# Every second one-hot matrix of the longest neighbour tile made by ScalarE instead of every fourth, with two changed distances in the instruction order

## The chip, the core and the metric

The kernel runs on one core of a Trainium2 chip. The core has five instruction queues that run side by side and each in its own order: TensorE (PE in the profile, with PEld for its weight loads), VectorE (DVE), ScalarE (ACT), GpSimd (POOL) and SyncE (SP, which only starts DMAs here). The metric is the device time of one execution in microseconds (us). Shown for the kernel before are 14 runs: median 7110.54 us, from 7096.17 to 7130.31 us.

## The reference: what is computed

There are 16 graphs of 1024 nodes, 64 features per node, a dense 1024x1024 weighted adjacency, and four layers, each ending in a residual addition and a layer normalisation. The first two layers are matrix products with the adjacency and a small perceptron. The last two, one after the other, do this for each node:

```
adj_d = adjacency with some neighbours taken out ("dilated", both directions)
vals  = x of the remaining neighbours of each node, sorted per feature
agg   = 0.25*q(0.25) + 0.5*q(0.5) + 0.25*q(0.75)     # interpolated quantiles
y     = (relu((x + agg) @ W1 + b1) @ W2 + b2) * mask
x     = layernorm(x + y)
```

A node has some ten to thirty neighbours left. So the heart of the work is: collect the neighbours' rows, sort them per feature, weigh three quantiles.

## The kernel before, in words

**Tiles.** For each graph the nodes are ordered by their number of neighbours and cut into eight tiles of 128 nodes. The tiles have fixed list lengths, `SIZES = (10, 11, 13, 14, 15, 17, 19, 33)` (L26); the last is the long tile. Rounds k = 0 to 17 pair graph k in its third layer (member 0) with graph k-2 in its fourth (member 1), so that both are sorted by the same VectorE instructions. Rounds 0, 1, 16 and 17 have one member.

**Short tiles (0 to 6).** GpSimd gathers neighbour rows from DRAM with indirect DMAs, one per list place, tile and member (`gather`, L361), into the buffer `got_s`, a ring of 60 places (`fetch`, L908). A gather can be issued when the places that it writes have been freed, that is, when an earlier tile has been sorted, weighed and added up.

**The long tile (7).** Its rows are not gathered but picked by TensorE (`fill`, L728; `pick`, L354). For list place i = 1 to 32 and each member, a one-hot matrix `hot` (128 x 1024, bf16) says where `place` equals i, and 24 pairs of weight load and matmul against the three bf16 parts of x write 64 columns of a PSUM tile `pgk`. Four places share half of `pgk`; ScalarE copies a half out to `got` (`empty`, L742) when the second place of the next four has been issued. Of each four one-hots three are made by VectorE, by one `is_equal`, and the one with i % 4 == 3 by ScalarE in two activations, `far = |place - i|` (L750) and `hot = relu(1 - far)` (L752); those are issued two places ahead. All one-hots take turns in `HOTS = 6` buffers, in the order in which they are asked for.

**Order of the work.** The order on VectorE, ScalarE and TensorE is written out by a small planner, `Weave` (L846). The sorting instructions of VectorE are the clock: `Metered` (L193) adds 0.13 us and one 960th of a us per element for each VectorE instruction, or one 3840th for a `tensor_scalar` whose large operands are all 16 bits wide. I call such a planned us a *unit*. All other work is written as generators; `yield n` means that the next piece is due n units later, times the work's pace. After every sorting instruction `catch_up` emits all pieces that have come due. `finish` forces a work to its end, and its due times no longer count then. The generators are: `features` (layers one and two), `lists` and `ordered` (neighbour lists, L486 and L633), `fill`, `weigh` (ScalarE multiplies the sorted places by weights, L773), and `finish_round` (L930), which runs the perceptron and normalisation (`finish`, L793, and `settle`, L371) of a round's members while the next round is sorted. `read_back` (L835) then loads the rewritten rows again.

A place of `fill` takes `yield 2.4`, so a fill is 31 x 2.4 = 74.4 units from its first one-hot to its last (the pace is 0.7 for k < 3). A round ends with the sort of its long tile.

In `finish`, each half of the perceptron is: transpose on TensorE, copy, first product, activation, second product `pd` (L816), then `yield 9` (L817) before VectorE adds `pd` to the bias.

Of the kernel before, what the change touches and what calls it, by code (L numbers as in the profile page):

```python
# [13 lines left out]
F16 = mybir.dt.float16  # L14
BF = mybir.dt.bfloat16
I32 = mybir.dt.int32
U8 = mybir.dt.uint8
AF = mybir.ActivationFunctionType
ALU = mybir.AluOpType
AX = mybir.AxisListType  # L20

P = 128
# [7 lines left out]
HOTS = 6  # L30
# [182 lines left out]
def adj_resnorm_kernel(ctx: ExitStack, tc: tile.TileContext, x, adj_t, nodemask, w01, b01, w02, b02,  # L213
                       w21, b21, w22, b22, w31, b31, w32, b32, out):
    nc = tc.nc
    B, N, C = x.shape
    NT = N // P
# [506 lines left out]
    def members(k):  # L724

        return [(m, b, entries[b]) for m, b in enumerate((k, k - 2)) if 0 <= b < B]

    def fill(k):  # L728

        while k and (k - 1, NT - 1) not in free:  # L730
            yield 1
        t = NT - 1
        size = SIZES[t]
        got = tails[k] = s.lists.tile([P, 2, size, C], F32, name="got", tag="got_l", bufs=1)
        for m, b, e in members(k):
            while e.parts[m] is None or e.xs[m] is None or e.place is None or e.none is None:
                yield 1
            nc.scalar.copy(got[:, m, 0, :], e.xs[m][:, t, :])
            waiting = None

            def empty():
                nc.scalar.copy(got[:, m, waiting[0] : waiting[0] + 4, :], waiting[1])  # L742

            for i in range(1, size):
                if i % 4 == 1:
                    first, pg = i, pgs[i // 4 % 2]
                if i % 4 == 1:

                    far = s.work.tile([P, NT, P], F16, name="far", bufs=1)
                    nc.scalar.activation(far, e.place, AF.Abs, bias=minus_k[:, i + 2 : i + 3])  # L750
                    by_act = s.lists.tile([P, NT, P], BF, name="hot", bufs=HOTS)
                    nc.scalar.activation(by_act, far, AF.Relu, bias=one_f, scale=-1.0)  # L752
                if i % 4 == 3:
                    hot = by_act
                else:
                    hot = s.lists.tile([P, NT, P], BF, name="hot", bufs=HOTS)
                    dve.tensor_scalar(hot, e.place, float(i), None, op0=ALU.is_equal)
                whole = i < LEAST[t]
                if not whole:
                    nc.tensor.matmul(pg[:, i - first, :], e.none,  # L760
                                     ident_b[: KW - 1, i - 1 : i].to_broadcast([KW - 1, C]), start=True, stop=False)
                pick(pg[:, i - first, :], hot, e.parts[m], whole)
                yield 2.4
                if i % 4 == 2 and waiting:
                    empty()
                if i % 4 == 0:
                    waiting = first, pg
            yield 5
            empty()
            yield 0.5  # L770
            e.filled[m] = True
# [21 lines left out]
    def finish(b, e, layer, agg):  # L793

        xc = e.xs[layer]
        w1s, b1c, w2s, b2r = mlps[layer]
        y = s.work.tile([P, NT, C], F32, name="y_m", bufs=1)
        dve.tensor_add(agg, agg, xc)
        yield 2
        for h in range(NH):  # L800
            pt = s.psum.tile([P, HALF], F32, name="pt", tag="m", bufs=1)
            for q in range(G):
                nc.tensor.transpose(pt[:C, q * P : (q + 1) * P], agg[:, h * G + q, :], ident)
            yield 7
            o_t = s.work.tile([C, HALF], F32, name="o_t", bufs=1)
            nc.scalar.copy(o_t, pt[:C])
            yield 3
            ph = s.psum.tile([P, HALF], F32, name="ph", tag="m", bufs=1)
            nc.tensor.matmul(ph[:H], w1s, o_t, start=True, stop=True)
            yield 7  # L810
            h_t = s.work.tile([H, HALF], F32, name="h_t", tag="o_t", bufs=1)
            nc.scalar.activation(h_t, ph[:H], AF.Relu, bias=b1c)
            yield 3
            pd = s.psum.tile([P, G, C], F32, name="pd", tag="m", bufs=1)
            for q in range(G):
                nc.tensor.matmul(pd[:, q, :], h_t[:, q * P : (q + 1) * P], w2s, start=True, stop=True)  # L816
            yield 9  # L817
            dve.tensor_add(y[:, h * G : (h + 1) * G], pd, b2r[:, None, :].to_broadcast([P, G, C]))
        dve.tensor_mul(y, y, e.mask[:, :, None].to_broadcast([P, NT, C]))
        dve.tensor_add(y, y, xc)  # L820
        xn = agg if layer else s.feat.tile([P, NT, C], F32, name="x3s", bufs=3)
        yield from settle(xn, y, "m")
        yield 1
        dst, rows = (out_rows_of, e.out_rows) if layer else (table[1][b % 3], e.rows)
        for t in range(NT):
            put = nc.gpsimd.indirect_dma_start(
                out=dst, out_offset=bass.IndirectOffsetOnAxis(ap=rows[:, t : t + 1], axis=0), in_=xn[:, t, :],
                in_offset=None)
            tc.declare_no_dep(put.ins, group=f"rows{layer}{b}", reason="they write different rows")
            tc.add_to_no_dep_group(f"rows{layer}{b}", put.ins)  # L830
        if layer == 0:
            e.xs[1] = xn
            weave.add(read_back(b, e, dst))
# [103 lines left out]
    def sort_round(k):  # L937

        if k >= 2:
            weave.finish(rounds[k - 2])  # L940
        filling = weave.add(fill(k), 4.0, 0.7 if k < 3 else 1.0)
        first = members(k)[0][0]
        which = slice(first, first + len(members(k)))
        agg = s.feat.tile([P, 2, NT, C], F32, name="agg")
        sums = []
        for t in (*reversed(range(NT - 1)), NT - 1):
            if t == NT - 1:
                weave.finish(filling)
                got = tails[k]
            else:  # L950
                n = order_of_tiles.index((k, t))
                fetch(n)
                got = gots[n]
            other = s.lists.tile([P, 2, SIZES[t], C], F32, name="other", bufs=1)
            pair = got[:, which], other[:, which]
            for is_max, d, v, i, j, to in usual[t]:
                dve.tensor_tensor(cut_pair(pair[to], v, d if is_max else 0), cut_pair(pair[i], v),
                                  cut_pair(pair[j], v, d), op=ALU.max if is_max else ALU.min)
                weave.catch_up()
                fetch()  # L960
            if len(sums) >= 2:
                weave.finish(sums[-2])
            sums.append(weave.add(weigh(k, t, got, agg, which)))
            weave.catch_up()
        if k:
            weave.finish(rounds[k - 1])
        rounds.append(weave.add(finish_round(k, agg, sums)))

    with ExitStack() as main:
        s.feat = main.enter_context(tc.tile_pool(name="feat", bufs=2))  # L970
# [305 lines left out]
```

## Time and profile before

| quantity | value |
|---|---|
| median of 14 runs | 7110.54 us |
| the profiled execution | 7098.59 us, with a span of 7096.8 us from first to last instruction |
| TensorE busy | 3917.4 us (55%) |
| VectorE busy | 4484.3 us (63%) |
| ScalarE busy | 2754.3 us (39%) |
| GpSimd busy | 3468.7 us (49%) |
| granted TensorE clock, mean | 0.682 |

No engine is full over the span, so the shares alone do not say what bounds. In the profile's groups of instructions, a row gives line, engine, operation, written tile and read tiles, shapes, count, then the busy time and the mean duration in ns, then the engine's idle time just before these instructions and what ended it. "issue" means that the engine waited for nothing that the profile shows; "remote" that the releasing instruction was not found. In the windows view each row is a stretch of the span with the busy time of each engine in it, and the number of instructions in brackets.

From round 3 on the rounds repeat almost exactly every 420 us. The stretch from 3062 to 3482 us is one of them: the fill of member 0 from 3062 to 3213 us, that of member 1 from 3213 to 3335 us, and from there to 3482 us the rest, with the sort of the long tile at its end.

### The profile page before, as it was taken

What the parts mean: (1) busy time and instruction counts of PE and PEld (TensorE: products, weight loads), DVE (VectorE), ACT (ScalarE), POOL (GpSimd) and SP (SyncE); (2) the same over time, 40 slices, a digit from 0 to 9 for tenths busy, and PEclk for the clock granted to TensorE, in tenths of its full rate; (3) what the DMA queues carried; (4) which work ended last, traced back from release to release, by engine and by line L of the source; (5) the groups of instructions that cost most, each with busy time, mean ns of one, the idle gap of its engine ahead of it and who ended that gap; (6) DMA issues with size and microseconds to landing.
All of it is one profiled execution on the core that took longest, in us unless ns stands there. A gap on an engine that the chain in (4) does not pass through costs nothing.

```text
span 7096.8 us, 109051 instructions
## 1 busy us (share of the span) xinstructions
PE 3917.4 (55%) x43478; PEld 2890.8 (41%) x43512; DVE 4484.3 (63%) x8771; ACT 2754.3 (39%) x6304; POOL 3468.7 (49%) x3229
## 2 busy tenths in 40 slices
PE   7657565465655656566565654746465564523233
PEld 5435344243443434444344443524344443413222
DVE  1456456657557485665858566585755748576666
ACT  4235153434435353443534334353443535322222
POOL 0342525546455464544645455464545646566353
PEclk8777676676766767676676766767676676755555
DMA  3111212111111111111111111111111111001000
GB/s 87 39 39 48 55 25 55 31 30 45 39 44 36 36 44 30 44 39 42 32 36 45 33 44 35 44 35 32 41 38 44 35 36 21 19 18 22 11 20 11
DMA packets 420598, 259.24 MB, mean 37 GB/s; under 512 B 106590, under 2 KB 368878, under 8 KB 420078
## 3 DMA queue, kind: packets, MB, share of 16 engines
q0 software_dynamic: 102400, 105.06, 7.9%
q1 hardware_dynamic: 317678, 147.12, 7.5%
q8 instruction: 342, 5.60, 0.3%
q14 instruction: 178, 1.46, 0.1%
HBM read 239.37 MB, written 12.58 MB: 36 GB/s over the span
## 4 chain that ended last, share of the span: by engine, by line
DVE 34%; PE 30%; issue 18%; another core or an unknown queue 11%; ACT 7%; POOL 0%; DMA 0%; DVEq 0%; ACTq 0%; POOLq 0%
DVE other L207 12%; PE pgk L358 11%; DVE got L207 7%; DVE got_s L207 6%; PE pk L607 5%; PE pa L465 3%; PE px L434 3%; DVE best L207 2%; PE ordered_x L358 1%; ACT junk L585 1%; PE pd L816 1%; DVE less L207 1%; DVE hot L207 1%; PE pr L520 1%
## 5 line engine op out<-in xcount | busy, mean ns | idle before, releaser
L362 POOL DMA_INDIRECT got_s<-table,idx x2944 | 3149.7, 1070 | 3348.0 <-DVE other L207 877.6
L358 PEld LDWEIGHTS <-hot 128*128 128x128 bf16 x24576 | 1092.5, 112 | 1817.4 <-issue 1477.7
L358 PE MATMUL pgk<-x3p,hot 128*128 128x64 bf16 x12288 | 691.1, 220 | 780.8 <-issue 483.3
L358 PE MATMUL pgk<-x2p,hot 128*128 128x64 bf16 x12288 | 619.7, 210 | 703.5 <-issue 437.0
L207 DVE TENSOR_SCALAR hot<-place 128x1024 bf16<-128x1024 f16 x768 | 335.0, 439 | 1038.7 <-remote 547.4
L742 ACT COPY got<-pgk 128x256 f32<-128x256 f32 x256 | 95.0, 371 | 2197.6 <-PE pgk L358 1518.7
L607 PE MATMUL pk<-near,order 128*128 128x512 f16 x2048 | 530.6, 413 | 44.0 <-issue 41.5
L520 PE MATMUL pr<-steps,near 128*128 128x512 bf16 x1502 | 423.1, 445 | 235.2 <-ACT junk L526 165.1
L207 DVE TENSOR_TENSOR other<-got_s 128x512 f32<-128x512 f32 (+8 forms) x900 | 511.5, 582 | 37.3 <-ACT got_s L925 17.5
L207 DVE TENSOR_TENSOR got_s<-got_s 128x384 f32<-128x384 f32 (+6 forms) x918 | 493.0, 539 | 21.1 <-DVE hot L207 0.9
L465 PE MATMUL pa<-x,adj_r 128*128 128x65 f32 x2048 | 395.1, 369 | 72.1 <-issue 35.8
L781 ACT ACTIVATE got_s<-got_s,wts 128x64 f32<-128x64 f32 x1568 | 398.9, 336 | 71.1 <-DVE got_s L207 55.2
L564 PE MATMUL pv<-minus_n,takes 128*128 128x128 bf16 x1024 | 248.6, 265 | 300.5 <-DVE takes L207 295.8
L207 DVE TENSOR_TENSOR got_s<-other 128x512 f32<-128x512 f32 (+8 forms) x774 | 407.5, 539 | 8.7 <-DVE other L207 0.8
L465 PEld LDWEIGHTS pa<-x,adj_r 128*128 128x128 f32 x2048 | 379.1, 284 | 73.9 <-issue 45.8
L520 PEld LDWEIGHTS <-near 128*128 128x128 f16 x1536 | 168.6, 111 | 482.6 <-issue 361.2
L563 PE MATMUL pv<-scaled,near 128*128 128x128 f16 x1024 | 250.1, 266 | 171.2 <-ACT near L568 164.8
L607 PEld LDWEIGHTS <-order 128*128 128x128 bf16 x2048 | 205.3, 105 | 322.6 <-issue 148.3
L434 PE MATMUL px<-adj_r,x_s 128*64 128x128 f32 x2048 | 310.2, 309 | 47.1 <-issue 41.9
L207 DVE TENSOR_TENSOR other<-other 128x128 f32<-128x128 f32 (+13 forms) x558 | 318.7, 571 | 17.4 <-issue 0.8
L564 PEld LDWEIGHTS <-takes 128*128 128x128 bf16 x1024 | 121.2, 118 | 500.7 <-DVE takes L207 327.0
L526 ACT ACTIVATE junk<-pr,nb_st 128x1024 f16<-128x1024 f32 x256 | 282.0, 1108 | 64.9 <-PE pr L520 63.0
(202 smaller groups left out, 7413.3 us busy)
## 6 DMA issues: line engine op xcount, KB each, us to landing
adj_r<-in_adj_dram SPq DMA_DIRECT2D x256, 512.0 KB
got_s<-table,idx POOLq DMA_INDIRECT x2944
x_s<-in_x_dram SPq DMA_DIRECT2D x16, 256.0 KB
table<-x SPq DMA_DIRECT2D x16, 256.0 KB
x<-table SPq DMA_DIRECT2D x16, 256.0 KB
table<-x3s,rows POOLq DMA_INDIRECT x128
out_dram<-agg,out_rows POOLq DMA_INDIRECT x128
table<-no_row SPq DMA_DIRECT2D x6, 0.2 KB
```

Of the source, the lines that this page charges most:

```text
L207: return call(*args, **kwargs)
L358: nc.tensor.matmul(dst, hot[:, c, :], parts[:, c, q, :], start=first and c + q == 0, stop=c == NT - 1 and q == 2)
L362: nc.gpsimd.indirect_dma_start(out=dst, out_offset=None, in_=tab, in_offset=bass.IndirectOffsetOnAxis(ap=rows, axis=0))
L434: nc.tensor.matmul(px[C:, q * P : (q + 1) * P], x_s[:, jt, :], adj[t][:, jt, :], start=jt == 0, stop=jt == NT - 1)
L465: nc.tensor.matmul(pa[:, q, :], adj[i][:, jt, :], x1[:, jt, :], start=jt == 0, stop=jt == NT - 1)
L520: nc.tensor.matmul(pr[:, h * HALF : (h + 1) * HALF], near[:, c, t * P : (t + 1) * P], steps[:, ONSET + h * HALF - c * P :][:, :HALF], star ...
L526: nc.scalar.activation(junk, prs[t - 1], AF.Sign, bias=lim[:, i, t - 1 : t], scale=-1.0, accum_out=cut_at[:, i, t - 1 : t])
L563: nc.tensor.matmul(pv[:, cols], near[:, c, rows], scaled[:, c, :], start=True, stop=False)
L564: nc.tensor.matmul(pv[:, cols], takes[:, c, rows], minus_n, start=False, stop=False)
L607: nc.tensor.matmul(cols, order[:, c, t * P : (t + 1) * P], left(c, slice(h * G, (h + 1) * G)), start=c == 0, stop=c == NT - 1)
L742: nc.scalar.copy(got[:, m, waiting[0] : waiting[0] + 4, :], waiting[1])
L781: nc.scalar.activation(prods[:, m, i, :], got[:, m, slot_id, :], AF.Copy, scale=e.wts[:, t, i : i + 1])
```

## The change

The one-hots of all odd places (i % 2 == 1) are made by ScalarE, 16 per fill instead of 8; VectorE makes 16 instead of 24. They are asked for up to two places ahead: at place 1 the order is hot 3, hot 1, hot 2; then 5, 4, 7, 6 and so on. In the perceptron's second product `yield 9` becomes `yield 13`. The `finish_round` of rounds 15, 16 and 17 gets a pace of 0.7 (lag 0.0 is the default).

```diff
+    def by_act(i):
+        return i % 2 == 1
...
+            hots = {}
+
+            def make(i):
+
+                hots[i] = s.lists.tile([P, NT, P], BF, name="hot", bufs=HOTS)
+                if by_act(i):
+                    far = s.work.tile([P, NT, P], F16, name="far", bufs=1)
+                    nc.scalar.activation(far, e.place, AF.Abs, bias=minus_k[:, i : i + 1])
+                    nc.scalar.activation(hots[i], far, AF.Relu, bias=one_f, scale=-1.0)
+                else:
+                    dve.tensor_scalar(hots[i], e.place, float(i), None, op0=ALU.is_equal)
+
             for i in range(1, size):
                 if i % 4 == 1:
                     first, pg = i, pgs[i // 4 % 2]
-                if i % 4 == 1:
-
-                    far = s.work.tile([P, NT, P], F16, name="far", bufs=1)
-                    nc.scalar.activation(far, e.place, AF.Abs, bias=minus_k[:, i + 2 : i + 3])
-                    by_act = s.lists.tile([P, NT, P], BF, name="hot", bufs=HOTS)
-                    nc.scalar.activation(by_act, far, AF.Relu, bias=one_f, scale=-1.0)
-                if i % 4 == 3:
-                    hot = by_act
-                else:
-                    hot = s.lists.tile([P, NT, P], BF, name="hot", bufs=HOTS)
-                    dve.tensor_scalar(hot, e.place, float(i), None, op0=ALU.is_equal)
+                for ahead in range(i + 1, min(i + 3, size)):
+                    if by_act(ahead) and ahead not in hots:
+                        make(ahead)
+                if i not in hots:
+                    make(i)
+                hot = hots[i]
...
-            yield 9
+            yield 13
             dve.tensor_add(y[:, h * G : (h + 1) * G], pd, b2r[:, None, :].to_broadcast([P, G, C]))
...
-        rounds.append(weave.add(finish_round(k, agg, sums)))
+        rounds.append(weave.add(finish_round(k, agg, sums), 0.0, 0.7 if k >= B - 1 else 1.0))
```

## The prediction

> **What bounds the kernel now.** I read the page's shares first, then the chain that ended last. No engine is full, and the chain changes hands all the time: a third is VectorE work, a third TensorE work, and 29% is time in which nothing named was waited for.
>
> ```profile
> PE 3917.4 (55%) x43478; PEld 2890.8 (41%) x43512; DVE 4484.3 (63%) x8771; ACT 2754.3 (39%) x6304; POOL 3468.7 (49%) x3229
> ...
> DVE 34%; PE 30%; issue 18%; another core or an unknown queue 11%; ACT 7%; POOL 0%; DMA 0%; DVEq 0%; ACTq 0%; POOLq 0%
> ```
>
> Second, one steady round of 420 us cut into the two fills and the rest (windows view; the 29 us left out lie between the last two rows).
>
> ```profile
> 3062.00:3213.00 151.00, 101.87 (x1265) 71.18 (x1265) 81.69 (x161) 54.66 (x109) 67.67 (x66) 0.76 0.15 33
> 3213.00:3335.00 122.00, 68.78 (x904) 58.93 (x903) 67.77 (x138) 39.84 (x92) 65.13 (x65) 0.67 0.17 40
> 3364.00:3482.00 118.00, 55.14 (x383) 34.08 (x384) 113.66 (x183) 75.15 (x189) 68.44 (x51) 0.69 0.16 37
> ```
>
> The third busy column is VectorE: about half full in the fills, full (113.66 of 118) after them. So the fills go at TensorE's pace and the rest at VectorE's. Third, the waits over the span:
>
> ```profile
> PEld L358 <- issue: 1511.4, 1364, 31.3
> ...
> DVE hot L207 <- remote: 547.4, 80, 23.3
> DVE hot L207 <- PE pgk L358: 482.0, 75, 21.8
> ...
> PE pgk L358 <- ACT got L742: 267.1, 80, 31.2
> ...
> DVE y_m L207 <- PE pd L816: 236.4, 33, 11.4
> ...
> DVE y_m L207 <- remote: 89.6, 10, 21.3
> ...
> PE pgk L760 <- ACT got L742: 79.2, 57, 9.4
> ```
>
> VectorE waits 1029 us for a free one-hot buffer, that is, for TensorE. TensorE, where its records show a gap, mostly waits for nothing ("issue"). The timeline shows when: while GpSimd issues gathers back to back, TensorE starts only a few instructions per us; elsewhere it does the 24 pairs of one place in 0.9 us (at 3213.2, for one).
>
> ```profile
> 3156.09 0.94 POOL L362 DMA_INDIRECT got_s<-table,idx  x1 [0.30 <-issue]
> ...
> 3157.20 0.32 PE L358 MATMUL pgk<-x2p,hot 128*128 128x64 bf16 x3 [1.17 <-issue]
> ...
> 3157.34 0.94 POOL L362 DMA_INDIRECT got_s<-table,idx  x1 [0.30 <-issue]
> ...
> 3157.93 0.23 PE L358 MATMUL pgk<-x2p,hot 128*128 128x64 bf16 x1 [0.41 <-issue]
> ```
>
> Whether the gathers cause this I can't show; they go together here.
>
> **The change, part by part.** The sum is made against the profiled execution (7098.59 us, of which 1.8 lie outside the span); it is 12 us below the median of the 14 runs, and I apply the difference to that median.
>
> ```profile
> L207 DVE TENSOR_SCALAR hot<-place 128x1024 bf16<-128x1024 f16 x768 | 335.0, 439 | 1038.7 <-remote 547.4 <-PE pgk L358 482.0 <-issue 8.9
> ...
> L750 ACT ACTIVATE far<-place,minus_k 128x1024 f16<-128x1024 f16 x256 | 294.5, 1150 | 2.9 <-DVE place L207 2.4
> L752 ACT ACTIVATE hot<-far,one_f 128x1024 bf16<-128x1024 f16 x256 | 294.0, 1148 | 9.9 <-remote 1.6
> ```
>
> (1) *VectorE loses work.* 32 fills x 8 = 256 one-hots x 335.0/768 = 0.436 us: 112 us. They stand in the fills, where VectorE has time, but the planner moves the gain: a one-hot counts 0.13 + 1024/3840 = 0.397 units, a fill stays 74.4 units long, so 3.2 units of sorting move into each fill and leave the full stretch, which runs at about one us per unit. 32 x 3.2 = 102 us. Bounds: 0 and 112. I take -102. The Trainium skill's page "Perfetto Trace Analysis" (Identifying Performance Opportunities) says that improving a kernel generally means improving its most-contended engine, which by occupancy is VectorE; by it alone the term would be the whole 112 and the forecast 10 us lower. The windows disagree: in the fills relief of VectorE buys nothing by itself.
>
> (2) *Sorting brings its gathers along.* In the round GpSimd works 219.5 us beside 274.9 us of VectorE (sums of the same view over 3062 to 3482), 0.8 us per us, so 3.2 units bring 2.55 us, or 3.4 us with the 0.30 gaps (1.25 us a gather for 0.94 busy). If TensorE stood still in all of it: 32 x 3.4 = 109 us back; if in none: 0. In the two fills TensorE's matmul row is idle 102 of 273 us; its waits for named instructions are 27 (16.1 for `got`, 7.0 for a one-hot, 4.2 for `junk`), so 75 us of standing beside 133 x 1.25/0.94 = 177 us of gather time, 42%. I take 42% of 109, +46.
>
> (3) *The first one-hot.* Place 1 was made by VectorE in 0.43 us; now ScalarE makes hot 3, then hot 1, and TensorE waits for the last of four activations.
>
> ```profile
> 3061.99 1.15 ACT L750 ACTIVATE far<-place,minus_k 128x1024 f16<-128x1024 f16 x1
> 3063.17 1.15 ACT L752 ACTIVATE hot<-far,one_f 128x1024 bf16<-128x1024 f16 x1
> ```
>
> At 1.18 us a piece the fourth ends at 3066.7; TensorE began the fill at 3062.3. That is 4.4 us later, with the next graph's `px` products (L434) queued behind. In a round's second fill TensorE came to place 1 only at 3221.9 us, when ScalarE's four would just have ended (from 3216.8), so 18 first fills count: 0 to 79 us. TensorE has 20 us a round of named waits later in the fills that can take up such a delay; I take a quarter, +20. If ScalarE were busy at that place, its backlog would come on top.
>
> (4) *Later odd one-hots.* 256 x 2.298 = 588 us more for ScalarE, 18.4 us a fill. It is busy 54.7 of 151 and 39.8 of 122 us there, so it fits; without that room it would cost all 588. But hot 4n+5 now stands in ScalarE's queue behind the copy of places 4n-3 to 4n, which waits for TensorE, and behind it stand copies, `junk` and `weigh` for VectorE. From that copy (0.37) and two activations (2.3) to TensorE's need lie four places, 4 x 0.9 us at its quickest. Lower bound 0; upper 2.3 each. The nearest row is the one-hots ScalarE makes now: TensorE waited 9.0 us in all for 256 (5.4 weight loads, 3.6 matmuls). I take the same, +9. The page "TensorE: Matmul & The Clock Gate" (Architectural detail) calls ScalarE's queue strict FIFO, so a late copy would hold each such one-hot: by that rule alone, as an estimate, 256 x up to 2.3, 589 us instead of 9. The trace bears the waiting out (`got` copies waited 1518.7 us for TensorE), but the lateness after it is not in it.
>
> (5) *Buffers.* With every fourth one-hot made early, VectorE's place 4n+2 needed the buffer of 4n-1: a reach of three places. Now an even place needs the buffer of six places earlier, a ScalarE one that of four before its time. VectorE's 155 buffer waits can shrink by 3 x 2.4 = 7.2 us each, but TensorE is behind there anyway and the next instruction waits (`deg`, 17.6 us at 3365). Bounds: 0 to -108 (half of 30 fills x 7.2). Taken: a part of the 346 us in which TensorE in turn waits for `got`, 1.5 us in 15 rounds, -22.
>
> (6) *Perceptron.* 43 waits of 326 us for `pd`, each at most 4 us shorter: up to -172, were they not in the fills (3119, 3193, 3317 us in this round), where the next one-hot would wait instead: 0. The end of each member's work moves 8 units back: its eight indirect DMAs on POOL's queue, and for member 0 the read-back on SP's. The next round's gathers need two more short tiles freed before that, and the fill needs the read-back a round later: nothing. Without that cover, 8 us x 14 rounds, 112 us.
>
> (7) *Last rounds.* A member's finish takes 87 units, now 95 x 0.7 = 66.5. Graph 15's rows, written from 6820 us, come up to 20 us earlier, so the last gathers (6834 to 6900) crowd the last fill (from 6870) less. Bounds -25 and +30 (16 shortened distances by up to 2 us); no wait for `pd` in that stretch is over 3.1 us, so the gain is nearer: -12.
>
> Sum: -102 + 46 + 20 + 9 - 22 + 0 - 12 = -61; 7110.5 - 61 gives 7050.
>
> **The rivals.** *The gathers take it all back:* (2) at its upper bound: -102 + 109 + 20 + 9 - 22 - 12 = +2, 7112 us. For it: the timeline above. Against it: 58% of gather time in the fills goes with TensorE running. *ScalarE becomes what TensorE waits for* (slower): place, hot 4n+5 and hot 1; price 0.3 us for each of the 256 (77) and the full 79 of (3): -102 + 46 + 79 + 77 - 22 - 12 = +66, 7177 us. It decides once both together exceed 90 us instead of my 29. For it: L781 and `junk` stand in the same queue. Against it: 9.0 us now. *The longer reach pays:* (5) at -108: 7050 - 86 = 6964 us. For it: 1029 us of buffer waits. Against it: no work for TensorE goes away.
>
> **How the numbers follow.** Forecast 0.50, its own range 6985 to 7095; gathers 0.14; ScalarE 0.24; reach 0.12. This kernel's runs tell about 0.2% (14 us) from no change. Faster: 0.48 + 0.03 + 0 + 0.12 = 0.63; same: 0.02 + 0.08 + 0.01 = 0.11; slower: 0.03 + 0.23 = 0.26. The range goes from 6930 (the reach's 6964 with (1) at 112 and (7) at -25, rounded down) to 7175, which leaves out about half of ScalarE's case and a third of the reach's.
>
> **What would show it.** (1) VectorE's one-hots x512, some 223 us; full stretch about 6 us shorter per round. (2) More "issue" beside the gathers in the fills. (3) and (4) In the waits, TensorE for `hot` L752-like rows from ScalarE: under 60 us right, over 120 us the ScalarE rival. (5) VectorE's waits for `hot` well under 1029 us, with others grown. (6) `pd` waits smaller, the round no shorter for it. (7) Gathers of the last round before 6815 us. I'd be wrong if a round of about 414 us doesn't appear, above all by a slower start of the fills.

## The result: slower by 1%

The changed kernel takes 7191.43 us (median of 10 runs, 7170.56 to 7208.3), the kernel before beside it 7119.73 us (47 runs): a ratio of 1.0099, with a 95% interval of 1.0082 to 1.0117. That is 72 us slower, clear of no change, where 61 us faster was forecast, and above the range's end of 7175. The profiled execution took 7164.88 us, with a span of 7163.2.

First the page's shares of the changed kernel, then its one-hot rows among the groups of instructions.

```profile
PE 3929.6 (55%) x43477; PEld 2913.8 (41%) x43512; DVE 4387.7 (61%) x8515; ACT 3316.7 (46%) x6816; POOL 3495.4 (49%) x3229
...
L207 DVE TENSOR_SCALAR hot<-place 128x1024 bf16<-128x1024 f16 x512 | 220.4, 431 | 1250.2 <-remote 657.4
L755 ACT ACTIVATE hot<-far,one_f 128x1024 bf16<-128x1024 f16 x512 | 587.9, 1148 | 16.7
...
L754 ACT ACTIVATE far<-place,minus_k 128x1024 f16<-128x1024 f16 x512 | 586.7, 1146 | 5.9 <-DVE place L207 2.4
```

The work moved as costed: VectorE's one-hots fell from 335.0 to 220.4 us (223 expected), ScalarE's rose by 586 us (588). VectorE is less busy and the kernel is slower. The waits of the changed kernel say who waits now (us in total, times, longest):

```profile
DVE hot L207 <- remote: 657.4, 65, 27.4
...
DVE hot L207 <- PE pgk L358: 554.4, 81, 28.7
...
PEld L358 <- ACT hot L755: 374.3, 61, 95.3
POOL table L836 <- ACT x3s L388: 358.8, 31, 27.1
...
DVE best L207 <- ACT code L618: 280.2, 31, 61.8
...
PE pgk L770 <- ACT got L745: 202.7, 61, 16.0
PE pgk L358 <- ACT got L745: 193.2, 71, 20.7
```

The rows of before that answer to these:

```profile
POOL got_s L362 <- ACT got_s L781: 514.5, 98, 14.8
...
PEld L358 <- DVE hot L207: 198.5, 28, 96.0
...
DVE best L207 <- ACT code L618: 93.0, 19, 59.3
POOL table L826 <- ACT x3s L388: 92.5, 25, 31.9
...
PEld L358 <- DVE agg L207: 88.8, 1, 88.8
```

Before, weight loads waited 5.4 us for ScalarE's one-hots and 198.5 for VectorE's; `best` waited 93.0 us for `code`, and GpSimd's writes into `table` 92.5 us for `x3s`. TensorE's waits for ScalarE's copy `got` have two rows: at `e.none`'s product (L760 before, L770 now) they rose from 79.2 to 202.7 us, at the one-hot products (L358) they fell from 267.1 to 193.2, together 346 before and 396 now. Two long waits, at the starts of the fills of rounds 15 and 16, are in both kernels and only change their names: before 96.0 us for a VectorE one-hot and 88.8 for `agg`, now both for a ScalarE one-hot:

```profile
6455.53 2.69 PE L358 MATMUL pgk<-x2p,hot 128*128 128x64 bf16 x47 [94.17 <-ACT hot L755]
```

```profile
6803.04 1.20 PE L358 MATMUL pgk<-x3p,hot 128*128 128x64 bf16 x19 [95.21 <-ACT hot L755]
```

Without these two TensorE's weight loads wait 185 us for ScalarE's one-hots, and 219 us for one-hots of both engines, where it was 108 before.

The steady round that answers to the one shown of before, as windows (length, then busy us of PE, PEld, DVE, ACT, POOL, granted clock, DMA share, GB/s): first fill, second fill, the rest.

```profile
3120.00:3273.00 153.00, 93.47 (x1200) 69.19 (x1201) 80.06 (x157) 69.24 (x118) 77.14 (x75) 0.71 0.16 35
3273.00:3403.00 130.00, 85.48 (x969) 68.66 (x968) 68.26 (x137) 62.34 (x117) 62.90 (x60) 0.62 0.15 36
3403.00:3540.00 137.00, 76.36 (x550) 54.39 (x551) 120.10 (x198) 75.60 (x192) 84.61 (x66) 0.65 0.19 44
```

Before: 151, 122 and 147 us. The rest is 10 us shorter (step (1) expected 6), and the fills are 10 us longer. The round is 420 us again, not 414. The granted clock is lower in this round, but over the span it is 0.679 against 0.682.

So the 66 us between the two traces are mostly not in the steady rounds. The starts of the fills, changed kernel minus before (from the first one-hot of each in the two traces):

```
fill (round)    2 (2)  4 (3)  8 (5)  14 (8)  20 (11)  26 (14)  31 (17)  end
whole change    +12    +13    +49    +58     +70      +54      +89      +66
```

49 us are lost before round 5, 5 us in the nine rounds after it, and the remaining 12 in the last rounds. I had costed one steady round and multiplied.

### The profile page after: what moved, and what is told of

Same layout as the page of the kernel before. It is cut to its first block, busy times and chain, and to the rows that moved or that the text cites. A ratio compares the mean times of both kernels' runs of the same rounds, so it can differ in the third digit from the quotient of the medians.

```text
span 7163.2 us, 109625 instructions
## 1 busy us (share of the span) xinstructions
PE 3929.6 (55%) x43477; PEld 2913.8 (41%) x43512; DVE 4387.7 (61%) x8515; ACT 3316.7 (46%) x6816; POOL 3495.4 (49%) x3229
## 5 line engine op out<-in xcount | busy, mean ns | idle before, releaser
L362 POOL DMA_INDIRECT got_s<-table,idx x2944 | 3177.3, 1079 | 3105.5 <-ACT got_s L791 794.9
L358 PEld LDWEIGHTS <-hot 128*128 128x128 bf16 x24576 | 1079.9, 112 | 1908.2 <-issue 1451.8
L358 PE MATMUL pgk<-x2p,hot 128*128 128x64 bf16 x12288 | 637.6, 213 | 754.3 <-issue 410.1
L358 PE MATMUL pgk<-x3p,hot 128*128 128x64 bf16 x12288 | 647.1, 216 | 631.2 <-issue 411.6
L207 DVE TENSOR_SCALAR hot<-place 128x1024 bf16<-128x1024 f16 x512 | 220.4, 431 | 1250.2 <-remote 657.4
L755 ACT ACTIVATE hot<-far,one_f 128x1024 bf16<-128x1024 f16 x512 | 587.9, 1148 | 16.7
L754 ACT ACTIVATE far<-place,minus_k 128x1024 f16<-128x1024 f16 x512 | 586.7, 1146 | 5.9 <-DVE place L207 2.4
L465 PE MATMUL pa<-x,adj_r 128*128 128x65 f32 x2048 | 425.9, 377 | 176.5 <-issue 149.8
L207 DVE TENSOR_TENSOR got_s<-got_s 128x256 f32<-128x256 f32 (+6 forms) x918 | 491.0, 538 | 34.8 <-remote 12.7
L465 PEld LDWEIGHTS pa<-x,adj_r 128*128 128x128 f32 x2048 | 409.0, 295 | 186.4 <-issue 158.5
L207 DVE MAX8 best<-code 128x8 f16<-128x1024 f16 x112 | 136.9, 1222 | 329.7 <-ACT code L618 280.2
L836 POOL DMA_INDIRECT table<-x3s,rows x128 | 142.3, 1112 | 388.9 <-ACT x3s L388 358.8
```

The source lines that it names most:

```text
L207: return call(*args, **kwargs)
L358: nc.tensor.matmul(dst, hot[:, c, :], parts[:, c, q, :], start=first and c + q == 0, stop=c == NT - 1 and q == 2)
L362: nc.gpsimd.indirect_dma_start(out=dst, out_offset=None, in_=tab, in_offset=bass.IndirectOffsetOnAxis(ap=rows, axis=0))
L465: nc.tensor.matmul(pa[:, q, :], adj[i][:, jt, :], x1[:, jt, :], start=jt == 0, stop=jt == NT - 1)
L755: nc.scalar.activation(hots[i], far, AF.Relu, bias=one_f, scale=-1.0)
L836: put = nc.gpsimd.indirect_dma_start(out=dst, out_offset=bass.IndirectOffsetOnAxis(ap=rows[:, t : t + 1], axis=0), in_=xn[:, t, :], in_off ...
```

## The experiments

The theories: *S*, ScalarE's share: what TensorE needs from ScalarE, one-hots and copies, comes later. *G*: the sorting and gathers that the planner moves into the fills cost more there than the rest of the round gains. *N*: the moving is worth nothing either way. *D*: the longer perceptron distance delays the next rows. Kernels that were run together share their chip and their runs of the kernel before. The chip matters, as will be seen, so each group names its time for the kernel before.

### The parts alone (kernel before: 7107.67 us)

**The one-hots alone**: the change with these two lines put back.

```diff
-            yield 13
+            yield 9
...
-        rounds.append(weave.add(finish_round(k, agg, sums), 0.0, 0.7 if k >= B - 1 else 1.0))
+        rounds.append(weave.add(finish_round(k, agg, sums)))
```

> The one-hots changed alone; the distance in the perceptron (9) and the pace of the last rounds (1.0) as before. Theory S (ScalarE: what TensorE waits for, and what else stands in ScalarE's queue, comes later): this part alone carries the loss, ratio 1.007 to 1.015, TensorE's waits for one-hots of ScalarE over 200 us. Theory D (the longer distance in the perceptron delays the rows of the next layer): ratio 0.990 to 1.002 here, since the one-hots by themselves would gain as forecast.

Measured 7215.18 us, ratio 1.0157 (1.0129 to 1.0184): +108 us. So the one-hots by themselves carry the loss, and more than all of it.

**The distance alone.**

```diff
-            yield 9
+            yield 13
```

> The distance 13 in the perceptron alone. Theory S: 0.997 to 1.003, the waits for the second product shorter and others longer by as much. Theory D: 1.006 to 1.015, with the GpSimd queue waiting longer for the rewritten rows (92.5 us before, 358.8 us after the whole change).

Measured 7047.89 us, ratio 0.9913 (0.988 to 0.9945): -60 us, and the quickest kernel of this study on such a chip. Theory D falls here. VectorE's waits for `pd` fall from 326 us to 21; others of its waits grow, that of `best` for `code` from 93 to 190 us and that of `counted` for `pn` from 47 to 164. In the steady rounds each second fill begins 5 to 15 us sooner after the first. The fills' starts run ahead from round 6 on: -20 us at fill 14, -56 at fill 26, -59 at the end.

**The last rounds' pace alone.**

```diff
-        rounds.append(weave.add(finish_round(k, agg, sums)))
+        rounds.append(weave.add(finish_round(k, agg, sums), 0.0, 0.7 if k >= B - 1 else 1.0))
```

> The pace 0.7 of the last three finish rounds alone. Both theories: nothing changes up to round 15; ratio 0.996 to 1.000, a gain of 0 to 25 us after 6700 us. If the last rounds carry the loss instead, 1.003 or more.

Measured 7104.91 us, ratio 1.0003 (0.9984 to 1.0022): no change that can be told from nothing.

**The one-hots alone, but place 1 made by VectorE**, so 17 of the 32 are VectorE's. In this expectation "272 more instead of 256 fewer" is a slip of mine: VectorE makes 17 x 32 = 544 instead of 768.

```diff
-        return i % 2 == 1
+        return i % 2 == 1 and i > 1
```

> As the one-hots alone, but place 1 of each fill is again made by VectorE (272 more instead of 256 fewer on VectorE: it makes 17 of 32, ScalarE 15). If the late start of the fills (4.4 us in each of the 18 first fills) is what costs, this gives back 40 to 80 us against the one-hots alone, ratio to before near 1.000. If the loss lies in ScalarE's queue within the fills, it gives back under 20 us.

Measured 7184.18 us, ratio 1.0104 (1.0079 to 1.013). Place 1 is worth 31 us of the 108 by the medians; the intervals of the two ratios just overlap, so the size is rough. The waits of this kernel show what it gained and what stayed:

```profile
POOL got_s L362 <- ACT got_s L791: 932.7, 112, 24.1
...
DVE best L207 <- ACT code L618: 272.1, 30, 63.6
...
PE pgk L770 <- ACT got L745: 163.1, 73, 17.2
...
PE pgk L358 <- ACT got L745: 158.6, 61, 7.6
...
PEld L358 <- DVE hot L207: 139.3, 46, 93.8
...
PEld L358 <- ACT hot L755: 72.1, 43, 4.5
```

Without the one wait of 94 us, TensorE's weight loads now wait 118 us for one-hots of both engines, against 108 us in the kernel before. So they wait hardly longer for the matrices than before, and 76 us of loss stay. What stays high is `best` for ScalarE's `code` (before 93.0), the gathers for ScalarE's weighing of `got_s` (before 514.5) and `table` for `x3s` (331.4, before 92.5). TensorE's waits for the copy `got` are not among them: their two rows make 322 us, less than the 346 before.

Multiplied, the three parts make 1.0157 x 0.9913 x 1.0003 = 1.0072; the whole was 1.0099. With the intervals given, that is consistent with adding up. By stage they don't add up: from fill 8 to fill 26 the one-hots alone lose 19 us against before and the distance alone gains 66, but the whole change loses 5.

### Less for VectorE, more for ScalarE, each alone (kernel before: 6930.8 us)

**224 of VectorE's one-hots left out** (places 5, 9, ... 29 reuse the matrix before).

```diff
-                else:
+                elif i % 4 != 1 or i == 1:
                     hot = s.lists.tile([P, NT, P], BF, name="hot", bufs=HOTS)
                     dve.tensor_scalar(hot, e.place, float(i), None, op0=ALU.is_equal)
```

> 224 of VectorE's 768 one-hots are left out of the kernel before (places 5, 9, ..., 29 reuse the matrix of the place before, so those places fetch the wrong neighbour); nothing goes to ScalarE. It is step (1) with step (2) and without (3) and (4). By the prediction's steps: 7/8 of -102 and 7/8 of +46, about -50 us, ratio 0.993. Theory N (the gain of step (1) is not there: the rest of a round shortens, and the fill grows by as much because TensorE's work and the gathers are what they were): ratio 0.998 to 1.002, and then all of the loss of the one-hots comes from ScalarE. Theory G (the gathers and the sorting that move into the fills cost more than VectorE saves): ratio above 1.003.

**The same, with the planner's clock kept.**

```diff
+                else:
+                    dve.us += 0.13 + NT * P / 3840
```

> The same 224 one-hots left out, but the planner's clock still counts 0.397 units for each, so no sorting and no gather moves into the fills; VectorE only has 98 us less to do there. By step (1) (relief of VectorE in the fills buys nothing by itself): ratio 0.997 to 1.003. If VectorE does hold the fills up (its waits for buffers notwithstanding): down to -98 us, ratio 0.986. Against the run without the clock it shows what the moving of sorting is worth: -50 us by the prediction, 0 by theory N, a loss by theory G.

Measured 7095.18 us, ratio 1.0238 (1.0204 to 1.0272), and 7002.44 us, ratio 1.0102 (1.0066 to 1.0137). Both leave 224 places with the wrong neighbours. The two kernels do the same work; they differ only in where the planner puts the sorting, and that costs 93 us. In their traces the stretches from first to last one-hot of all fills sum to 4112 us against 3921, and all the rest to 2983 against 3075. So the rest of the rounds shortened by 92 us, where step (1) says 7/8 of 102, that is 90; and the fills grew by 191, where step (2) says 7/8 of 46, that is 40. The waits of the first kernel, with the moving:

```profile
POOL got_s L362 <- ACT got_s L781: 906.5, 102, 22.6
...
DVE best L207 <- ACT code L618: 283.8, 24, 61.5
...
DVE counted L207 <- PE pn L692: 257.3, 15, 39.0
```

and of the second, without it:

```profile
POOL got_s L362 <- ACT got_s L783: 424.5, 88, 15.1
...
DVE best L207 <- ACT code L618: 75.2, 19, 19.4
...
DVE counted L207 <- PE pn L692: 69.4, 17, 6.8
```

The reading that fits: with more sorting in the same 74.4 units, VectorE reaches steps that need TensorE (`code` comes from the product `pk`, `pn` is a transpose) before TensorE, which is behind in a fill, has done them, and stands in front of its own sorting. The first two rows are raised in the changed kernel, too (794.9 and 280.2 us). The time is theory G on this chip. What I can't explain is the second kernel: 98 us less work, nothing moved, and 72 us slower. I have no trace of the kernel before from this chip to compare.

**The one-hots on ScalarE, with the planner's clock kept.**

```diff
+                    if i % 4 == 1:
+                        dve.us += 0.13 + NT * P / 3840
```

> The one-hots alone as in the change, but the planner's clock counts 0.397 units for each of the 256 that ScalarE makes more, so the order of all other work is nearly that of before. The one-hots alone measured 1.0157. By the prediction's steps the gain of (1) and the cost of (2) both go: 56 us more than with the one-hots alone, ratio about 1.023. Theory N: the same as the one-hots alone, 1.013 to 1.018. Theory G: a good part of the loss goes, ratio 1.002 to 1.009.

Measured 7073.86 us, ratio 1.0209 (1.0181 to 1.0238). Against the kernel with fewer one-hots and the clock kept, making them on ScalarE costs another 71 us, place 1 included (it moves 256 one-hots, the other leaves out 224). The one-hots alone weren't run on this chip, so what the moving costs *them* here stays open.

**More work for ScalarE that nobody reads.**

```diff
+                if i % 4 == 3 and i + 2 < size:
+                    far = s.work.tile([P, NT, P], F16, name="far", bufs=1)
+                    nc.scalar.activation(far, e.place, AF.Abs, bias=minus_k[:, i + 2 : i + 3])
+                    nc.scalar.activation(far, far, AF.Relu, bias=one_f, scale=-1.0)
```

> The kernel before with 224 more pairs of activations on ScalarE (Abs and Relu, 128 x 1024, 515 us in all) at the places of the fill where the change issues those of the odd one-hots; nothing reads what they make. It shows what the room in ScalarE's queue is worth without TensorE needing the result. By step (4) (it fits, 39% busy): ratio 0.998 to 1.002. Theory L (what else stands in the queue, copies, code and weighing, comes later by up to 2.3 us each): ratio 1.005 to 1.012. If the loss of the one-hots lies in TensorE's need for the matrix itself, this run shows next to none of it.

Measured 6987.0 us, ratio 1.0097 (1.0066 to 1.0129): 56 us for 515 us of work in an engine that is 39% busy. That is theory L, and against step (4)'s "it fits". But the kernel with less work lost as much on this chip, so I don't take the number for ScalarE's alone: something that costs any edited program 1% there is not excluded.

The traces do say which waits go with the moved sorting. Waits in us, first of `best` for `code`, then of the gathers for the weighing of `got_s`, then of `table` for `x3s`:

| kernel | sorting moved | more for ScalarE | `best` | gathers | `table` |
|---|---|---|---|---|---|
| before | no | no | 93 | 515 | 93 |
| the distance 13 alone | no | no | 190 | 588 | 115 |
| one-hots alone | yes | yes | 242 | 795 | 405 |
| place 1 by VectorE | yes | yes | 272 | 933 | 331 |
| fewer one-hots | yes | no | 284 | 907 | 366 |
| fewer, clock kept | no | no | 75 | 425 | 106 |
| one-hots, clock kept | no | yes | 45 | 660 | 134 |
| more work that nobody reads | no | yes | 39 | 445 | 112 |

The upper four ran on the chips of 7100 us, the lower four on that of 6931. The waits for `code` and `x3s` are long where the sorting is moved, with more work for ScalarE or without it. So where they stay high with place 1 by VectorE, the likely reason is the moving and not ScalarE's added work. The gathers wait longer for the weighing with the moving, and with the one-hots on ScalarE. What these waits cost in time, the table doesn't say.

### The same program without TensorE's gaps (kernel before: 5172.2 us)

**The kernel before, for a trace.**

> The kernel before itself, for a trace from the chip of the runs beside it: the four runs with fewer one-hots and with more work for ScalarE were on a chip on which the kernel before took 6931 us, 2.5% less than where its trace was made. Expected: a span within 0.5% of the kernel before's median here, ratio 0.995 to 1.005.

Measured 5170.87 us. On this chip the same program takes 27% less time. Its shares, rows and waits:

```profile
PE 3422.6 (66%) x43478; PEld 2639.5 (51%) x43512; DVE 4470.3 (86%) x8771; ACT 2755.1 (53%) x6304; POOL 3635.7 (70%) x3229
...
L362 POOL DMA_INDIRECT got_s<-table,idx x2944 | 3320.6, 1128 | 1345.1 <-issue 684.6
...
L207 DVE TENSOR_SCALAR hot<-place 128x1024 bf16<-128x1024 f16 x768 | 343.4, 452 | 32.5 <-PE pgk L358 32.5
```

```profile
PEld L358 <- DVE hot L207: 656.4, 239, 100.5
...
PEld L358 <- issue: 146.1, 186, 5.8
```

TensorE's weight loads stand in "issue" 146 us instead of 1511, the fills sum to 2499 us instead of 3972, and VectorE waits 33 us for one-hot buffers instead of 1029. A one-hot or a gather takes no less time than before (452 against 439 ns, 1128 against 1070). VectorE is now the fullest engine: 86% busy over the span, and 67.4 of 69 us in the second fill of a steady round. And beside gathers that follow each other as closely as on the first chip, TensorE does the 24 pairs of a place in 0.88 us:

```profile
3125.91 0.94 POOL L362 DMA_INDIRECT got_s<-table,idx  x1 [0.30 <-DMA got_s<-table,idx]
3127.16 1.03 POOL L362 DMA_INDIRECT got_s<-table,idx  x1 [0.30 <-DMA got_s<-table,idx]
```

```profile
3127.23 0.88 PE L358 MATMUL pgk<-x2p,hot 128*128 128x64 bf16 x24 [1.67 <-DVE hot L207]
```

So the issuing of gathers alone doesn't make the gaps.

**The one-hots alone, and with the planner's clock kept, here.**

> The one-hots alone, beside the same with the planner's clock kept. If the chip plays no part: ratio 1.013 to 1.019 again. If a chip on which the kernel before is quick has less room for the loss: the ratio is larger there, 1.02 to 1.035. Theory G (sorting and gathers that move into the fills cost more than the rest of the round gains, as 1.0238 against 1.0102 with fewer one-hots says) expects this kernel to be slower than the next one on the same chip, by some 0.5% to 1.3%; theory N expects the two the same within 0.3%.

> The one-hots on ScalarE with the planner's clock counting 0.397 units for each, on the same chip as the run above. Theory G: 0.5% to 1.3% quicker than the one-hots alone. Theory N: the same. By the prediction's steps (1) and (2): 56 us (0.8%) slower than the one-hots alone.

Measured 5219.78 us, ratio 1.0096 (1.0081 to 1.0112), and 5326.65 us, ratio 1.0291 (1.0277 to 1.0305). Here the moving *gains* 107 us: step (1)'s term, almost to the number, with theories G and N both wrong on this chip. But it doesn't come from where step (1) puts it: in rounds 0 to 13 the fills are 79 us shorter for the moving and the rest 51, where step (1) has the whole gain in the rest. From the starts of the fills (this kernel minus before):

```
fill (round)          2 (2)  4 (3)  8 (5)  14 (8)  20 (11)  26 (14)  31 (17)  end
one-hots alone        +21    +25    +30    +26     +30      +31      +48      +46
with the clock kept   +28    +44    +48    +85     +123     +160     +155     +156
```

A steady round is 295 us before, 295 with the one-hots alone, 307 with the clock kept. So ScalarE's one-hots cost 12 us a round, the moved sorting gives 12 back, and the loss that is left lies in the first rounds and the last ones, as for the whole change on the chip with gaps. One place where ScalarE costs time is in the timeline of the one-hots alone, ScalarE's queue first, then TensorE's matmuls:

```profile
3253.64 0.99 ACT L618 CAST code<-pk 128x1024 f16<-128x1024 f32 x1
3254.54 2.02 ACT L378 ACTIVATE y_x<-y_x,ln_st_x 128x64 f32<-128x64 f32 x8
3256.59 0.63 ACT L379 ACTIVATE x<-y_x 128x512 f32<-128x512 f32 x1
3257.12 0.35 ACT L745 COPY got<-pgk 128x256 f32<-128x256 f32 x1
3257.37 1.15 ACT L754 ACTIVATE far<-place,minus_k 128x1024 f16<-128x1024 f16 x1
3258.55 1.15 ACT L755 ACTIVATE hot<-far,one_f 128x1024 bf16<-128x1024 f16 x1
```

```profile
3252.25 2.96 PE L358 MATMUL pgk<-x3p,hot 128*128 128x64 bf16 x96
3257.53 1.56 PE L358 MATMUL pgk<-x3p,hot 128*128 128x64 bf16 x48 [2.31 <-ACT got L745]
3259.76 1.57 PE L358 MATMUL pgk<-x3p,hot 128*128 128x64 bf16 x48 [0.67 <-ACT hot L755]
```

ScalarE works without a break here. Its copy `got`, which frees half of `pgk`, stands behind a `code` and a normalisation; TensorE waits 2.31 us for the copy, then 0.67 for the one-hot behind it. ScalarE is busy 60.5 of 77 us in this fill (38.2 of 69 before); on the average over the span it is far from full.

**A distance of 17.**

```diff
-            yield 9
+            yield 17
```

> The kernel before with the distance before the perceptron's last addition 17 instead of 9 (13 alone measured 0.9913). Step (6) priced the 13 at nothing, because the next one-hot would wait instead. If the gain comes from VectorE no longer standing for the perceptron's product in the fills, it was all taken with 13 and 17 gives the same, 0.988 to 0.995. If the gain comes from where the sorting lands, 17 need not keep it: anything from 0.985 to 1.005. If the longer distance delays the next round's rows: above 0.995.

Measured 5247.72 us, ratio 1.0158 (1.0142 to 1.0173): slower. As this chip has no gaps, and 13 alone loses here, too (below), the run doesn't tell where 13's gain with gaps came from.

### All together, still without gaps (kernel before: 5165.89 us, then 5169.75 us)

> The whole change, on one chip with its parts. If its parts add up: the ratio of the one-hots alone times the ratio of 13 alone (the last rounds alone measured 1.0003), within 0.4%. Where the kernel before takes about 7100 us: 1.008 to 1.012 again. On a chip without TensorE's issue gaps (before near 5170 us): the one-hots alone gave 1.0096 there, and VectorE is busy 86%, so 13 has less to hide behind: 1.005 to 1.025.

> The one-hots alone: 1.0157 where before took 7108 us, 1.0096 where it took 5172 us. Expected near the one or the other by the chip's time for the kernel before.

> The one-hots on ScalarE with the planner's clock kept: 1.0291 where before took 5172 us (the one-hots alone 1.0096 there: the planner's move was worth 107 us, the 102 of step 1), 1.0209 where it took 6931 us. Theory A (where TensorE stands in issue gaps, what moves into the fills costs there what the rest gains): the same as the one-hots alone, within 0.4%, where before takes 6900 to 7200 us. Theory G (it costs more than the rest gains): 0.5% or more below the one-hots alone. Step (1) as predicted: 0.8% above.

> The distance 13 alone: 0.9913 where before took 7108 us. Theory C (the gain is VectorE's waits for the perceptron's product, 326 us of them in the kernel before, in fills that wait for TensorE): the same again there, 0.988 to 0.995; on a chip without TensorE's gaps those waits are 137 us in the kernel before, and the gain is 0 to -0.6%, unless the later rows cost as 17 did there (1.0158): 1.000 to 1.010.

Measured: the whole change 5235.22 us, ratio 1.0128 (1.0108 to 1.0148); the one-hots alone 1.0115 (1.0098 to 1.0132); with the clock kept 1.0287 (1.0272 to 1.0302), so the moving is worth 91 us; 13 alone 1.0074 (1.0058 to 1.0089). The distance that gains 60 us where TensorE has gaps costs 41 here. The waits for `pd` that it removes are 137 us here, and they do fall, to 22; other waits of VectorE grow: for the DMA of the adjacency (24 to 101 us) and for a one-hot buffer (33 to 89). The product of the parts is 1.0190, the whole 1.0128: here they don't add up.

**No gathers**, for what the gaps hang on, and the clock kept once more.

```diff
-                        gather(got[:, m, i, :], table[m][b % 3], e.idx[:, t, i - 1 : i])
+                        nc.gpsimd.memset(got[:, m, i, :], 0.0)
```

> The kernel before with each of the 2944 gathers replaced by a GpSimd memset of the same slot to zero, so the sorting sorts zeros; queues, waits and the order of everything else are kept, no gather's DMA is issued. Where the kernel before shows TensorE's issue gaps (7100 us): if the gathers are needed for the gaps, the weight loads' issue waits of 1511 us fall under 300 us and the time falls to 5000 to 5400 us; if they are not, the waits stay above 1000 us and the time above 6700 us. Where the kernel before takes 5170 us there are no gaps to lose: 4700 to 5150 us, less GpSimd work alone.

> The one-hots with the planner's clock kept. Where before takes 7050 to 7200 us: theory G (the moved sorting costs more in the fills than the rest gains) 1.002 to 1.010, against 1.0157 for the one-hots alone; theory A 1.012 to 1.019; step (1) as predicted 1.023. Where before takes 6930 us: 1.0209 again; where it takes 5170 us: 1.029 again.

Measured 5031.98 us, ratio 0.9732 (0.9714 to 0.975), and 5320.99 us, ratio 1.0283 (1.0269 to 1.0297). There were no gaps here to lose, so the first run tells only that with memsets (347 us of GpSimd) for all 2944 gathers (3321 us) the kernel takes 138 us less. Whether the gaps need the gathers stays open.

## Why the prediction was wrong

**What bounds the kernel.** "The fills go at TensorE's pace and the rest at VectorE's" fits the chips with gaps, and is a property of those chips: without gaps VectorE fills up in the fills, too (75.0 of 88 and 67.4 of 69 us in a steady round, 81.7 of 151 and 67.8 of 122 with gaps).

The two steps that failed, (2) and (4), are about what TensorE stands for in the fills. So here are, for rounds 0 to 13 of each trace, the lengths of the fills and of the rest, and the times over 0.15 us in the fills in which neither a matmul nor a weight load ran, summed by what ended them (us):

| kernel | fills | rest | TensorE stands | "issue" | copy `got` | ScalarE's one-hots | VectorE's one-hots |
|---|---|---|---|---|---|---|---|
| before | 3275 | 2458 | 1106 | 889 | 202 | 2 | 3 |
| last rounds alone (the same order so far) | 3269 | 2458 | 1096 | 891 | 189 | 2 | 2 |
| whole change | 3405 | 2381 | 1305 | 850 | 259 | 144 | 20 |
| one-hots alone | 3384 | 2407 | 1253 | 854 | 234 | 127 | 0 |
| place 1 by VectorE | 3444 | 2350 | 1250 | 1007 | 157 | 62 | 15 |
| fewer, clock kept (6931 us) | 3249 | 2389 | 1086 | 892 | 183 | 3 | 2 |
| fewer one-hots (6931 us) | 3410 | 2320 | 1239 | 817 | 350 | 55 | 14 |

The second row says how well such sums repeat.

**Step (1), VectorE loses work: right with gaps.** In these rounds the rest is 78 us shorter in the changed kernel, where the step makes it 83 (26 fills); it is 51 with the one-hots alone, and over the whole span of fewer one-hots 92 where the step makes it 90. Without gaps the totals agree, 107 and 91 us, but half or more of them came out of the fills, so there the agreement is luck.

**Step (2), sorting brings gathers along: a step that failed.** Forecast +46, at most 109, from TensorE standing in "issue" beside 42% of the gather time that moves in. The gathers did move in: in rounds 0 to 13 the fills of the changed kernel hold 84 us more of gather time (1948 to 2032 us, gaps of up to 0.6 us counted in), where the step makes it 88. But TensorE's standing in "issue" there, the sign that I had set, did not grow: 889 to 850 us, and 892 to 817 where the moving is tried by itself. Yet the moving by itself lengthened all fills by 191 us where 40 were forecast. What grew in its place are waits for named instructions, which the step put at nothing: TensorE's for ScalarE's copy `got` (183 to 350 us) and for its one-hots (3 to 55), VectorE's in front of `best` and `counted`, and the gathers' for ScalarE's weighing (424.5 to 906.5 us over the span). In the changed kernel's steady round the fills took back all of the 10 us that the rest gained.

**Step (3), the first one-hot: right in kind, 31 us for the 20.** But not "18 first fills" alike: place 1 by VectorE gains 16 us up to round 5 against the one-hots alone, loses 20 in rounds 5 to 13 and gains 39 after them.

**Step (4), later odd one-hots: failed too, in its size.** I took +9 from how little TensorE waited for a ScalarE one-hot before, and 20 for place 1. In the table TensorE stands 144 us for ScalarE's one-hots in the fills of the changed kernel, against 2; over the span its weight loads wait 185 us for them without the two long waits, against 5.4. An average of 54.7 busy us in 151 did not say that a one-hot is ready when it is needed. The Trainium skill's page "TensorE: Matmul & The Clock Gate" (Architectural detail) calls ScalarE's queue strict FIFO, which I set aside at this step because the trace showed no lateness. The timeline above agrees with it: the one-hot stands behind the late copy, and TensorE waits 2.31 us for the copy and 0.67 for the one-hot. How much of the 76 us that stay with place 1 by VectorE is ScalarE's queue isn't shown: the waits for `code` and `x3s` that stay high there go with the moved sorting elsewhere, and TensorE's standing in "issue" is longer by 118 us in that trace. ScalarE's price by itself is 12 us a round without gaps; with gaps the two runs for it say 71 us (against fewer one-hots with the clock kept) and 56 us (idle load), both on a chip where even less work was slower, so this is no firm number.

**Step (5), the buffers' reach: no sign of it.** VectorE's waits for a one-hot buffer were to fall well under 1029 us; they are 1212. It was not tried alone.

**Step (6), the perceptron: forecast 0, measured -60.** It lies inside my bounds (-172 to +112), but "the next one-hot would wait instead" is wrong where there are gaps: VectorE's buffer waits are 976 us with 13, not longer than the 1029 before. Waits for `code` and `pn` grew instead, by 214 us together, and the kernel was quicker all the same; where the 60 us come from is not shown. The one-hots alone lost 1.57%, the whole change 0.99%.

**Step (7), the last rounds: forecast -12, measured -3**, and its interval includes no change.

**The rival that came nearest** is ScalarE's, which I priced at 7177 us and gave 0.24: TensorE's waits for ScalarE's one-hots passed 120 us, the sign that I had set. Its sum was near, partly by luck, for its parts were not: place 1 costs some 31 us, not 79, the moved sorting of step (2) has a part in the rest, and the gain of step (6) hides some 40 us of the loss in the result.

**The multiplication.** Each term was a steady round or fill times 14 to 32. Nearly all the loss of the whole change lies in rounds 0 to 4 and 14 to 17; the one-hots alone lose 40 us in rounds 0 to 4, 19 in rounds 5 to 13 and 60 after them. In the fill of round 1 (626 to 715 us in the changed kernel) ScalarE is busy 76 of 89 us (59 of 87 before): the pace gives a place 1.7 units there instead of 2.4.

**What stays open.** On a chip with gaps the one-hots alone and the same with the clock kept were not run side by side; 1.0157 and 1.0209 come from chips of 7108 and 6931 us. So of their 108 us some 31 go to place 1, and how the remaining 76 divide into the moved sorting and ScalarE's queue is not known. Why leaving work out and adding idle work both cost 1% on the chip of 6931 us is not known either.

## What to carry to other kernels

An engine's busy share over the span says nothing about room in the stretch where you put the work: look at its busy time in that stretch, at what already stands in its queue, and at who waits for the copies behind it. Where an order is planned by one engine's clock, taking work from that engine also moves everything else; run the edit once with the clock kept, to see the two apart. And cost the first and last rounds by themselves, above all where the spacing is different there.

No version here that does the whole work beats both kernels everywhere: the distance of 13 alone is the best with gaps (0.9913, on the one such chip where it ran), the kernel before without them.

## What the runs showed of the hardware

The same program took 7108, 6931, 5172 and 5170 us on four chips, each time repeatable within about 1%, with the same instructions and, in the two traces of it, nearly the same durations of one-hots and gathers (439 and 452 ns, 1070 and 1128 ns). The difference that shows is TensorE's "issue": in the slow trace of before it mostly starts at most four matmuls and then pauses, four times in five for 0.3 to 1.2 us, mostly while indirect DMAs are issued (1334 us of such pauses beside them, 293 apart from them); in the quick trace it hardly does (39 and 72 us), though indirect DMAs are under way in 89% of the span there (61% in the slow one, counting gaps between them of up to 0.6 us). The mean granted clock is 0.755 there and 0.682 on the slow one. What makes the difference is not in the trace: the instruction queue of the DMA (342 packets, 5.60 MB) moved the same in the same time (375 and 369 us of packets). Whether it belongs to the chip or to the session can't be told from one or two sessions each. For a verdict on such a kernel it means that it holds for one kind of chip: 13 is a gain of 0.9% on one and a loss of 0.7% on the other.
